# One written order of the engines from the feed-forward through the attention, with the first scores and softmax weights inside the feed-forward's end

## The chip, the cores and the metric

The kernel runs on one core of a Trainium2 chip. A core has five engines with queues of their own: PE (TensorE, matrix products into the accumulator banks of PSUM), DVE (VectorE), ACT (ScalarE), POOL (GpSimd) and SP (SyncE, which here only issues transfers). Each engine works through its queue in order and waits on semaphores for the others; sixteen DMA engines move data between DRAM and the on-chip memory. The metric is the device time of the whole kernel in microseconds (us), the median of several runs; lower is better.

## The reference

Two layers of a gated cross-attention network work on x, 4 sequences of 512 rows of 512 numbers (16 tiles of 128 rows). Each of four stages adds `tanh(gate) * f(layernorm(x))` to x:

1. a gated product with the context, whose "expert" is chosen by a row's token number;
2. a feed-forward in which rows, weights and hidden values are rounded in blocks of 32 to a small float format: `down(q(silu(gate(q(h))) * up(q(h))))`, with 2048 hidden columns;
3. an attention in which queries are the normalised x, keys and values are the context, with 8 heads that each cover 64 of a sequence's 512 rows and attend over the 512 columns: `softmax(q k / 8) v`;
4. a mixture of 64 experts, 6 per row, with at most 96 rows per expert, and a shared expert.

The change touches the end of stage 2 and stage 3.

## The kernel before, in words

**Framework.** Tiles come from pools with a number of buffers; a tile whose buffers are in use waits for a release, and a pool that opens where a closed one lay waits for what was in it. Inside `tc.manual_schedule(engines=...)` the named engines keep the order of the program; elsewhere a scheduler with an estimate of times orders them at compile time. SP is always ordered by the scheduler, and so are DMA issues on it.

**Feed-forward (lines 611 to 806).** One manual block over PE, ACT, DVE and POOL. Per tile j: `normal` (ACT) makes h; `block_scales` and `block_round` (DVE, with a wide cast on ACT, L638) round it; `turned_rows` transposes it (PE, L668, with a copy on ACT, L669); `gate_up(j, c)` computes 512 columns of gate and of up for c = 0 to 3 (PE, L688), each in a PSUM bank of its own from `ps_g` (4 banks); `silu` (ACT, L698) reads the gate bank, `times_up` (DVE, L702) multiplies with the up bank; the 1024 columns of a half are rounded and transposed (`turned_hidden`); `down` (PE, L708) makes y; `add_rows` scales it (ACT, L713) and POOL adds it to x_rows in DRAM (L714). The loop interleaves two tiles: `turned_hidden(j - 1, 1)` and `down(j - 1)` run in the round of tile j. `row_sums` on ACT (L150: an Identity and a Square pass, each with a sum) and `row_factors` on DVE give the normalisation, four tiles at a time.

**Queries of the attention.** `query_moments` uses DVE instead: `bn_stats`, `bn_aggr`, and per group three Newton steps (`newton`) for the inverse root. Groups are tiles 0 and 1, 2 and 3, then fours; the first two groups lie in rounds 13 and 14 of the feed-forward. `query(0)` (ACT) closes round 14.

**Attention (lines 831 to 1156).** A second manual block, over PE, ACT and DVE. Step n is quarter i of tile j: `scores` (PE, L850, two heads into a two-bank tile at_s, two such tiles), `highest` (DVE, L855), `weights` (ACT, L864, exponentials p, with their sums), and two steps later `turned` (PE transposes of p, L874, and copies on ACT to pT, L875). p lies in the pool `at`, which is opened after the feed-forward's pools are closed. `values`, `weighted` and `attended` of tile j - 1 follow within tile j; `attended` also sends x_tile to out (L920), and `row` makes the router's input. `fetch` loads rows of the context (c_tile, 3 buffers), `fetch_rows` loads x_rows (x_tile, 6 buffers). Expert weights are loaded on SP meanwhile (`load_expert`, L816 to L819), the first once the feed-forward's weights are done with.

**Experts.** After the attention the scheduler orders all engines again.

The functions which the change and the prediction name:

Of the kernel before, what the change touches and what calls it, by code (L numbers as in the profile page):

```python
# [9 lines left out]
F32 = mybir.dt.float32  # L10
# [4 lines left out]
ALU = mybir.AluOpType  # L15
# [4 lines left out]
P = 128  # L20
# [26 lines left out]
def flamingo_kernel(  # L47
# [101 lines left out]
            waste = pool.tile([P, D], F32, name="waste", bufs=1)  # L149
            nc.scalar.activation(waste, rows, f, bias=rows[:, 0:1], scale=-1.0, accum_out=sums[:, k, i : i + 1])  # L150

    def row_factors(small, sums, tiles):

        n = len(tiles)
        mean = small.tile([P, 2, n], F32, name="ln_mean", tag=f"ln_mean{n}")
        nc.vector.tensor_scalar(mean, sums, 1.0 / D, None, ALU.mult)
        a = small.tile([P, n], F32, name="ln_a", tag=f"ln_a{n}")
        nc.vector.scalar_tensor_tensor(a, mean[:, 0, :], -1.0, mean[:, 0, :], ALU.mult, ALU.mult)
        nc.vector.scalar_tensor_tensor(a, a, EPS, mean[:, 1, :], ALU.add, ALU.add)
        y = newton(a, small=small)  # L160
        shift = small.tile([P, n], F32, name="ln_shift", tag=f"ln_shift{n}")
        for i, rows in enumerate(tiles):
            nc.vector.scalar_tensor_tensor(
                shift[:, i : i + 1], mean[:, 0, i : i + 1], rows[:, 0:1], y[:, i : i + 1], ALU.subtract, ALU.mult
            )
        return [(y[:, i : i + 1], shift[:, i : i + 1]) for i in range(n)]
# [414 lines left out]
        nc.vector.bn_stats(st, tiles[j]["x"])  # L581
        nc.vector.bn_aggr(mv, st)

    query_groups = [[0, 1], [2, 3], [4, 5, 6, 7], [8, 9, 10, 11], [12, 13, 14, 15]]
    queries_of = {j: g for g in query_groups for j in g}

    def query_moments(j):
# [17 lines left out]
    def query(j):  # L605
        q = early.tile([P, D], F32, name="q")
        normalized(q, tiles[j]["x"], tiles[j].pop("first"))
        tiles[j]["q"] = q


    with (
        tc.tile_pool(name="ffn", bufs=2) as fp,
        tc.tile_pool(name="ffn_few", bufs=4) as few,
        tc.tile_pool(name="ps_g", bufs=4, space=PSUM) as ps_g,
        tc.tile_pool(name="ps_a", bufs=2, space=PSUM) as ps_a,
        tc.tile_pool(name="ps_h", bufs=1, space=PSUM) as ps_h,
        tc.tile_pool(name="ps_y", bufs=1, space=PSUM) as ps_y,
        tc.manual_schedule(engines={PE, ACT, DVE, POOL}),
    ):
        stages = [{} for _ in range(NT)]  # L620

# [59 lines left out]

        def gate_up(j, c):
            hT = stages[j]["hT"]
            got = []
            for wT in (wgT, wuT):
                ps = ps_g.tile([P, 512], F32, name="gu", tag="g")
                for k in range(KC):
                    nc.tensor.matmul(ps, hT[:, k, :], wT[:, k, bass.ts(c, 512)], start=k == 0, stop=k == KC - 1)  # L688
                got.append(ps)
            stages[j]["gu", c] = got  # L690

        def silu(j, c):

# [15 lines left out]
            stages[j]["y"] = y  # L709

        def add_rows(j):
            y_sb = fp.tile([P, D], F32, name="y_sb")
            nc.scalar.mul(y_sb, stages[j].pop("y"), tg_f0_256)  # L713
            nc.gpsimd.dma_start(x_rows[bass.ts(j, P), :], y_sb, accum_op=ALU.add)  # L714

# [36 lines left out]
        for j in range(NT):  # L752
            more = j + 1 < NT

            if j:
                turned_hidden(j - 1, 1)
            times_up(j, 0)
            times_up(j, 1)
            gate_up(j, 2)
            silu(j, 2)  # L760
            block_scales(j, ("a", 0), half_n)
            block_round(j, ("a", 0), half_n)
            gate_up(j, 3)
            silu(j, 3)
            if j:
                down(j - 1)
            if j + 8 < NT:
                load(j + 8)
            sums_of(j + 6)
            if j + 2 < NT:  # L770
                normal(j + 2)
            if more:
                block_scales(j + 1, "h", D)
                block_round(j + 1, "h", D)
            if j:
                add_rows(j - 1)
            if more:
                turned_rows(j + 1)
            turned_hidden(j, 0)
            if more:  # L780
                gate_up(j + 1, 0)
                silu(j + 1, 0)
            times_up(j, 2)
            times_up(j, 3)
            block_scales(j, ("a", 1), half_n)
            if more:
                gate_up(j + 1, 1)
                silu(j + 1, 1)
            block_round(j, ("a", 1), half_n)
            factors_from(j + 3)  # L790

            if j == NT - 6:
                for i in range(2):
                    fetch(i)
                for i in range(6):
                    fetch_rows(i)
            if j == NT - 3:
                query_moments(0)
                query_moments(1)
            if j == NT - 2:  # L800
                query_moments(2)
                query_moments(3)
                query(0)
        turned_hidden(NT - 1, 1)
        down(NT - 1)
        add_rows(NT - 1)
    mx_pool.__exit__(None, None, None)

# [23 lines left out]
    tp = at_pool.__enter__()  # L832
    with (
        tc.tile_pool(name="rt", bufs=2, side="right") as ap,
        tc.tile_pool(name="ps_s", bufs=2, space=PSUM) as ps_s,
        tc.tile_pool(name="ps_u", bufs=2, space=PSUM) as ps_t,
        tc.tile_pool(name="ps_o", bufs=2, space=PSUM) as ps_m,
        tc.manual_schedule(engines={PE, ACT, DVE}),
    ):
        first_w = ap.tile([P, KC, E + 2 * F], F32, name="first_w", bufs=1)  # L840

        def scores(j, i):
            t = tiles[j]
            if i == 0:
                t["pT"] = [tp.tile([P, KC, D], F32, name=f"pT{h}", bufs=1) for h in range(2)]
                t["sums"] = tp.tile([P, KC, 2], F32, name="sums")
            s = ps_s.tile([P, 2, D], F32, name="at_s")
            for h in range(2):
                rows = bass.ts(h, HD)
                nc.tensor.matmul(s[:, h, :], t["q"][rows, bass.ts(i, P)], t["c"][rows, :], start=True, stop=True)  # L850
            t["s", i] = s

        def highest(j, i):
            low = small.tile([P, 2], F32, name="low")
            nc.vector.tensor_reduce(low, tiles[j]["s", i], AX.X, ALU.max, negate=True)  # L855
            tiles[j]["low", i] = low

        def weights(j, i):

            t = tiles[j]  # L860
            s, low = t.pop(("s", i)), t.pop(("low", i))
            p = tp.tile([P, 2, D], F32, name="p", bufs=3)
            for h in range(2):
                nc.scalar.activation(  # L864
                    p[:, h, :], s[:, h, :], AF.Exp, bias=low[:, h : h + 1], accum_out=t["sums"][:, i, h : h + 1]
                )
            t["p", i] = p

        def turned(j, i):
            p = tiles[j].pop(("p", i))  # L870
            for h in range(2):
                ps = ps_t.tile([P, KC, P], F32, name="p_ps", tag="t")
                for k in range(KC):
                    nc.tensor.transpose(ps[:, k, :], p[:, h, bass.ts(k, P)], ident)  # L874
                nc.scalar.copy(tiles[j]["pT"][h][:, :, bass.ts(i, P)], ps)  # L875
# [20 lines left out]
        def bank(among, n, name):  # L896

            if among:
                return ps_m.tile([P, n], F32, name=name, tag="m")
            return ps_s.tile([P, 2, D], F32, name="at_s")[:, 0, :n]  # L900

        def values(j):
            pT = tiles[j].pop("pT")
# [170 lines left out]
        for n in range(NT * KC):  # L1074
            j, i = divmod(n, KC)
            turn = divmod(n - 2, KC)
            if i == 2:
                do(query, j + 1)
                do(weighted, j - 1)
            elif i == 3:  # L1080
                do(squashed, j - 2)
            scores(j, i)
            highest(j, i)
            do(turned, *turn)
            weights(j, i)
            if i == 0:
                do(turned_row, j - 2)
                do(over_sums, j - 1)
                do(shared_hidden, j - 3)
                do(groups_of, j - 3)  # L1090
                do(noted, j - 4, range(3))
                do(fetch, j + 2)
                if j >= 2:
                    do(fetch_rows, j + 4)
            elif i == 1:
                do(spread_sums, j - 1)
                do(experts_of, j - 3)
                do(values, j - 1)
                do(kept, j - 3)
                do(noted, j - 4, range(3, TOPK))  # L1100
                if j + 4 < NT:
                    query_moments(j + 4)
            elif i == 2:
                do(counted, j - 3)
                do(attended, j - 1)
                do(first_layer, j - 2)
                if j < ew.bufs:
                    load_expert(j, ew)
            else:
                do(slots, j - 3)  # L1110
                do(row, j - 1)
# [42 lines left out]
        noted(z, range(TOPK))  # L1154
        for j in range(z - 2, NT):
            shared_hidden(j)
    with (
        tc.tile_pool(name="ex", bufs=2) as xp,
        tc.tile_pool(name="ew3", bufs=2, side="right") as ew3,
# [146 lines left out]
```

## Time and profile before

| what | us |
|---|---|
| median of 3 runs (1237.53 to 1246.21) | 1242.14 |
| profiled execution | 1243.6 |
| its span, first to last instruction | 1241.3 |
| PE busy | 1019.4 (82%) |
| DVE busy | 798.3 (64%) |
| ACT busy | 566.2 (46%) |
| last transposes of the feed-forward (PE, L668) | start at 518.32 |
| third score step of the attention (PE, L850) | starts at 534.68 |

In rows of the timeline the columns are start, duration, engine, line, operation, output from input, shapes and count; in brackets stands the idle time of the engine before the row and what ended it. "PEld" is a weight load, "SPq" a queue's issue. In the chain of waits the columns are start, duration and what. A row of the view by stages begins with the stretch and its length, then busy us and instructions of PE, PEld, DVE, ACT and POOL, the granted PE clock, the DMA share and GB/s.

### The profile page before, as it was taken

The page shows a single profiled execution, that of the slowest core. Times are in us where ns is not written, and L with a number is a line of the kernel's source. Part 1 is how long each engine was busy: PE and PEld are TensorE (multiplying, and loading weights), DVE is VectorE, ACT ScalarE, POOL GpSimd, SP SyncE. Part 2 cuts the span into 40 slices and gives each one's busy share as a digit, 9 for nine tenths or more (in the row PEclk, how much of TensorE's full clock was granted, in tenths as well). Part 3 has the DMA queues.
Part 4 walks back from the last instruction along what each step waited for, and adds up shares of the span by engine and source line. Part 5 has one row for each costly group of instructions (what it writes and reads, how often), then busy time and mean ns, then how long its engine had stood idle before and what let it go on. Part 6 is the DMA issues. An engine that isn't in the chain of part 4 may idle for free.

```text
span 1241.3 us, 14865 instructions
## 1 busy us (share of the span) xinstructions
PE 1019.4 (82%) x4603; PEld 515.6 (42%) x4603; DVE 798.3 (64%) x1993; ACT 566.2 (46%) x1128; POOL 380.0 (31%) x526
## 2 busy tenths in 40 slices
PE   4489999637888787679999999971899999999993
PEld 4244454313333343234444444430455555544441
DVE  7799999949999999636878887762232222222231
ACT  3666674446767664366666666630111112111120
POOL 3123222100000000000544544554444444444424
PEclk9689999859999999989999999985899999999997
DMA  8934533331221111186221111027899999999978
GB/s 309 338 85 103 121 82 86 44 117 35 51 43 26 18 23 14 39 221 182 62 65 59 53 62 46 19 73 220 236 279 280 274 265 273 273 270 278 276 194 137
DMA packets 75804, 174.74 MB, mean 141 GB/s; under 512 B 13024, under 2 KB 14064, under 8 KB 75664
## 3 DMA queue, kind: packets, MB, share of 16 engines
q1 hardware_dynamic: 51696, 128.04, 34.6%
q0 software_dynamic: 23200, 45.16, 18.8%
q8 instruction: 37, 0.61, 0.2%
q10 hardware_dynamic: 832, 0.62, 0.2%
q14 instruction: 39, 0.32, 0.1%
HBM read 133.76 MB, written 44.20 MB: 143 GB/s over the span
## 4 chain that ended last, share of the span: by engine, by line
DVE 37%; PE 29%; DMA 20%; ACT 6%; issue 5%; POOL 1%; SPq 0%; DVEq 0%; POOLq 0%; ACTq 0%
DMA more_rows<-e_o,idx 13%; PE gu_ps L1196 5%; DVE mx_top L633 4%; PE e_y L1219 3%; PE first_ps L959 3%; PE at_o L907 3%; DVE inter L702 3%; DVE mx_q L649 3%; DVE low L855 3%; PE at_s L850 3%; PE l_mm L474 3%; PE p_ps L874 2%; DVE w_q L263 2%; DVE mx_c L656 2%; DVE w_src L260 2%
## 5 line engine op out<-in xcount | busy, mean ns | idle before, releaser
L1196 PE MATMUL gu_ps<-e_gu,gT 128*96 128x384 f32 x512 | 178.2, 491 | 0.0
L1200 DVE SCALAR_TENSOR_TENSOR a<-s,xg,gu_ps 96x192 f32<-96x192 f32 x64 | 35.0, 548 | 150.3 <-ACT s L1198 145.7
L1219 PE MATMUL e_y<-e_dn,eaT 96*96 96x512 f32 x256 | 120.5, 592 | 0.1
L123 POOL DMA_INDIRECT taken<-token_no,to_i x96 | 96.7, 1007 | 50.2 <-issue 24.3
L855 DVE TENSOR_REDUCE low<-at_s 128x2 f32<-128x1024 f32 x64 | 77.8, 1215 | 48.5 <-PE at_s L850 48.5
L1196 PEld LDWEIGHTS gu_ps<-e_gu,gT 128*96 128x96 f32 x512 | 79.2, 165 | 62.5 <-issue 62.2
L864 ACT ACTIVATE p<-at_s,low 128x512 f32<-128x512 f32 x128 | 87.4, 693 | 28.2 <-DVE low L855 25.1
L1188 DVE COPY gT<-g_ps 128x384 f32<-128x384 f32 x64 | 35.7, 558 | 96.8 <-PE g_ps L1186 91.6
L714 POOL DMA_DIRECT2D x_rows<-y_sb x16 | 13.7, 856 | 269.2 <-ACT y_sb L713 269.2
L1221 ACT COPY e_o<-e_y 96x512 f32<-96x512 f32 x64 | 37.2, 581 | 127.3 <-PE e_y L1219 64.4
L875 ACT COPY pT<-p_ps 128x512 f32<-128x512 f32 x128 | 70.7, 596 | 33.1 <-PE p_ps L874 32.1
L491 POOL DMA_INDIRECT x_rows<-y_sb,to_row x19 | 36.5, 1921 | 154.6 <-ACT y_sb L490 154.6
L850 PE MATMUL at_s<-c_tile,q 64*128 64x512 f32 x256 | 73.8, 655 | 11.2 <-ACT p L864 10.6
L1173 POOL DMA_INDIRECT xg<-h_rows,idx x64 | 59.9, 935 | 72.5 <-DVE a L1200 36.4
L874 PEld LDWEIGHTS p_ps<-ident,p 128*128 128x128 f32 x512 | 55.9, 143 | 59.0 <-issue 22.9
L874 PE MATMUL p_ps<-ident,p 128*128 128x128 f32 x512 | 74.8, 286 | 6.7 <-ACT hT L952 5.8
L688 PEld LDWEIGHTS <-hT 128*128 128x128 bf16 x512 | 49.8, 101 | 73.4 <-issue 17.1
L474 PE MATMUL l_mm<-cT,sT 128*128 x152 | 79.9, 674 | 0.3 <-ACT sT L461 0.3
L1198 ACT ACTIVATE s<-gu_ps 96x192 f32<-96x192 f32 x64 | 20.9, 326 | 123.0 <-PE gu_ps L1196 118.1
L688 PE MATMUL gu<-wgT,hT 128*128 128x512 bf16 x256 | 70.8, 402 | 6.1 <-ACT hT L669 6.1
L688 PE MATMUL gu<-wuT,hT 128*128 128x512 bf16 x256 | 68.1, 390 | 5.3 <-DVE inter L702 5.3
L668 PE MATMUL q_ps<-ident_bf,mx_c 128*128 128x128 bf16 x320 | 26.0, 233 | 56.1 <-DVE mx_c L656 41.1
(239 smaller groups left out, 2044.2 us busy)
## 6 DMA issues: line engine op xcount, KB each, us to landing
e_gu<-in_L_ffn_w_gate_dram SPq DMA_DIRECT2D x64, 384.0 KB
e_gu<-in_L_ffn_w_up_dram SPq DMA_DIRECT2D x64, 384.0 KB
e_dn<-in_L_ffn_w_down_dram SPq DMA_DIRECT2D x64, 384.0 KB
w_src<-in_L_ffn_w_gate_dram SPq DMA_DIRECT2D x8, 512.0 KB
c_sb<-in_ctx_dram SPq DMA_DIRECT2D x4, 1024.0 KB
w_src<-in_L_ffn_w_up_dram SPq DMA_DIRECT2D x8, 512.0 KB
more_rows<-zeros SPq DMA_DIRECT2D x16, 256.0 KB
w_src<-in_L_ffn_w_down_dram SPq DMA_DIRECT2D x8, 512.0 KB
```

The source lines that it names most:

```text
L123: ins = nc.gpsimd.indirect_dma_start(out=table[:, :], out_offset=bass.IndirectOffsetOnAxis(ap=to, axis=0), in_=what, in_offset=None)
L474: nc.tensor.matmul(ps.unsqueeze(1), aT[:, k, :], cT[:, bass.ds(at + k, 1), :], start=k == 0, stop=k == KC - 1)
L633: nc.vector.tensor_reduce(top, s3, AX.X, ALU.max, apply_absolute_value=True)
L688: nc.tensor.matmul(ps, hT[:, k, :], wT[:, k, bass.ts(c, 512)], start=k == 0, stop=k == KC - 1)
L850: nc.tensor.matmul(s[:, h, :], t["q"][rows, bass.ts(i, P)], t["c"][rows, :], start=True, stop=True)
L855: nc.vector.tensor_reduce(low, tiles[j]["s", i], AX.X, ALU.max, negate=True)
L864: nc.scalar.activation(p[:, h, :], s[:, h, :], AF.Exp, bias=low[:, h : h + 1], accum_out=t["sums"][:, i, h : h + 1])
L874: nc.tensor.transpose(ps[:, k, :], p[:, h, bass.ts(k, P)], ident)
L875: nc.scalar.copy(tiles[j]["pT"][h][:, :, bass.ts(i, P)], ps)
L1173: nc.gpsimd.indirect_dma_start(out=g[:, :], out_offset=None, in_=h_rows[:, :], in_offset=bass.IndirectOffsetOnAxis(ap=idx[:, e : e + 1], a ...
L1196: nc.tensor.matmul(ps, gT[:, k, :], gu[:, :, k, :], start=k == 0, stop=k == KC - 1)
L1219: nc.tensor.matmul(y, aT[:, c, :], dn[:, c, :], start=c == 0, stop=c == 1)
```

## The change

- One `manual_schedule` over PE, ACT and DVE spans the feed-forward and the attention; POOL is in no manual block any more.
- `ps_s` (two tiles of two banks) is opened ahead of both stages and replaces `ps_g`: gate and up of one `gate_up` share a tile, which the attention's scores use too.
- `scores`, `highest` and `weights` move ahead of the feed-forward; p and the sums lie in the pool `early`. Steps 0 and 1 of tile 0 are written between the last operations of the feed-forward, and left out of the attention's loop.
- The last tile's y_sb is a c_tile buffer of `early`.
- The moments of tiles 0 to 3 become `row_sums` on ACT in rounds 12 and 13 and one `row_factors` for four tiles in round 14, with the factor 1/8 handed on to `newton`.

```diff
-    def row_factors(small, sums, tiles):
+    def row_factors(small, sums, tiles, scale=None):
...
-        y = newton(a, small=small)
+        y = newton(a, scale, small=small)
...
-    query_groups = [[0, 1], [2, 3], [4, 5, 6, 7], [8, 9, 10, 11], [12, 13, 14, 15]]
+    query_groups = [[4, 5, 6, 7], [8, 9, 10, 11], [12, 13, 14, 15]]
...
+    def scores(j, i):
+        t = tiles[j]
+        if i == 0:
+            t["sums"] = early.tile([P, KC, 2], F32, name="sums")
+        s = ps_s.tile([P, 2, D], F32, name="at_s", tag="s")
...
+    def weights(j, i):
...
+        p = early.tile([P, 2, D], F32, name="p", bufs=3)
...
+    order = tc.manual_schedule(engines={PE, ACT, DVE})
+    order.__enter__()
+    score_banks = tc.tile_pool(name="ps_s", bufs=2, space=PSUM)
+    ps_s = score_banks.__enter__()
...
-        tc.tile_pool(name="ps_g", bufs=4, space=PSUM) as ps_g,
...
-        tc.manual_schedule(engines={PE, ACT, DVE, POOL}),
...
-            got = []
-            for wT in (wgT, wuT):
-                ps = ps_g.tile([P, 512], F32, name="gu", tag="g")
+            ps = ps_s.tile([P, 2, 512], F32, name="gu", tag="s")
+            for i, wT in enumerate((wgT, wuT)):
...
-            y_sb = fp.tile([P, D], F32, name="y_sb")
+            if j < NT - 1:
+                y_sb = fp.tile([P, D], F32, name="y_sb")
+            else:
+                y_sb = early.tile([P, D], F32, name="c_tile", bufs=3)
...
-            if j == NT - 3:
-                query_moments(0)
-                query_moments(1)
+            if j == NT - 4:
+                sums = few.tile([P, 2, 4], F32, name="ln_sums", tag="ln_sums4")
+            if NT - 4 <= j < NT - 2:
+                for i in range(2):
+                    t = 2 * (j - NT + 4) + i
+                    row_sums(fp, tiles[t]["x"], sums, t)
             if j == NT - 2:
-                query_moments(2)
-                query_moments(3)
+                for t, s in enumerate(row_factors(small, sums, [tiles[t]["x"] for t in range(4)], 1.0 / HD**0.5)):
+                    tiles[t]["first"] = s
                 query(0)
+            if j == NT - 1:
+                scores(0, 0)
+                scores(0, 1)
+        highest(0, 0)
         turned_hidden(NT - 1, 1)
+        weights(0, 0)
+        highest(0, 1)
         down(NT - 1)
+        weights(0, 1)
         add_rows(NT - 1)
...
-            scores(j, i)
-            highest(j, i)
+
+            if n >= 2:
+                scores(j, i)
+                highest(j, i)
             do(turned, *turn)
-            weights(j, i)
+            if n >= 2:
+                weights(j, i)
...
+    score_banks.__exit__(None, None, None)
+    order.__exit__(None, None, None)
```

More of the change, by code (lines that the diff above doesn't have):

```diff
@@ L608, in query, with highest @@
         tiles[j]["q"] = q
+    def scores(j, i):
[3 more added lines that the diff above has]
+        s = ps_s.tile([P, 2, D], F32, name="at_s", tag="s")
+        for h in range(2):
+            rows = bass.ts(h, HD)
+            nc.tensor.matmul(s[:, h, :], t["q"][rows, bass.ts(i, P)], t["c"][rows, :], start=True, stop=True)
+        t["s", i] = s
+    def highest(j, i):
+        low = small.tile([P, 2], F32, name="low")
+        nc.vector.tensor_reduce(low, tiles[j]["s", i], AX.X, ALU.max, negate=True)
+        tiles[j]["low", i] = low
+    def weights(j, i):
+        t = tiles[j]
+        s, low = t.pop(("s", i)), t.pop(("low", i))
+        p = early.tile([P, 2, D], F32, name="p", bufs=3)
+        for h in range(2):
+            nc.scalar.activation(
+                p[:, h, :], s[:, h, :], AF.Exp, bias=low[:, h : h + 1], accum_out=t["sums"][:, i, h : h + 1]
+            )
+        t["p", i] = p
+    order = tc.manual_schedule(engines={PE, ACT, DVE})
+    order.__enter__()
+    score_banks = tc.tile_pool(name="ps_s", bufs=2, space=PSUM)
+    ps_s = score_banks.__enter__()
     with (
@@ L683, in gate_up @@
             hT = stages[j]["hT"]
-            got = []
-            for wT in (wgT, wuT):
-                ps = ps_g.tile([P, 512], F32, name="gu", tag="g")
+            ps = ps_s.tile([P, 2, 512], F32, name="gu", tag="s")
+            for i, wT in enumerate((wgT, wuT)):
                 for k in range(KC):
-                    nc.tensor.matmul(ps, hT[:, k, :], wT[:, k, bass.ts(c, 512)], start=k == 0, stop=k == KC - 1)
-                got.append(ps)
-            stages[j]["gu", c] = got
+                    nc.tensor.matmul(ps[:, i, :], hT[:, k, :], wT[:, k, bass.ts(c, 512)], start=k == 0, stop=k == KC - 1)
+            stages[j]["gu", c] = ps[:, 0, :], ps[:, 1, :]
         def silu(j, c):
@@ L834, in flamingo_kernel, with turned @@
         tc.tile_pool(name="rt", bufs=2, side="right") as ap,
-        tc.tile_pool(name="ps_s", bufs=2, space=PSUM) as ps_s,
         tc.tile_pool(name="ps_u", bufs=2, space=PSUM) as ps_t,
         tc.tile_pool(name="ps_o", bufs=2, space=PSUM) as ps_m,
-        tc.manual_schedule(engines={PE, ACT, DVE}),
     ):
         first_w = ap.tile([P, KC, E + 2 * F], F32, name="first_w", bufs=1)
-        def scores(j, i):
-            t = tiles[j]
+        def turned(j, i):
             if i == 0:
[L845 to L869, printed above, removed]
+                tiles[j]["pT"] = [tp.tile([P, KC, D], F32, name=f"pT{h}", bufs=1) for h in range(2)]
             p = tiles[j].pop(("p", i))
@@ L899, in bank @@
                 return ps_m.tile([P, n], F32, name=name, tag="m")
-            return ps_s.tile([P, 2, D], F32, name="at_s")[:, 0, :n]
+            return ps_s.tile([P, 2, D], F32, name="at_s", tag="s")[:, 0, :n]
         def values(j):
```

## The prediction

> **What bounds the kernel now.** I read the page's slices first: PE's row falls to 7, 6 and 7 tenths in the three slices from 465 to 558 us, where the feed-forward hands over to the attention. The chain of waits over that stretch says why:
>
> ```profile
> 510.58 1.29 DVE inter L702 x2
> ...
> 514.80 1.14 DVE low L855
> 515.94 0.60 DVE mx_c L655
> 516.59 0.99 issue
> 517.59 0.69 DVE mx_c L656
> 518.32 0.62 PE q_ps L668 x8
> 518.94 5.15 PE y L708 x16
> 524.12 0.70 ACT y_sb L713
> ...
> 525.10 6.70 DMA x_rows<-y_sb
> 531.89 1.28 ACT L864
> 533.18 1.46 ACT p L864 x4
> 534.68 2.08 PE at_s L850 x4
> ...
> 554.08 10.65 DMA out_dram<-x_tile
> 564.80 2.62 DMA x_tile<-x_rows
> ```
>
> Columns: start, us, what. The two score maxima (low) are already computed at 514.7, inside the last rounding, and delay it. The exponentials (p) stand ready from 518 on but wait for the last feed-forward rows to be added in DRAM, then for a table load; PE's third score step waits for them until 534.68. Twenty us later DVE waits 5.2 us for x_tile 6, whose buffer is free only when out of tile 0 has landed.
>
> Then the timeline of DVE, ACT, PE and SP, for durations and slack:
>
> ```profile
> 482.09 0.69 DVE L581 BATCH_NORM_STATS2 st<-x_tile 128x6 f32<-128x512 f32 x1
> 486.47 1.28 DVE L702 TENSOR_TENSOR inter<-inter,gu 128x512 f32<-128x512 f32 x2
> ```
> ```profile
> 274.98 0.71 ACT L150 ACTIVATE waste<-xt 128x512 f32<-128x512 f32 x1
> 275.59 0.19 ACT L150 ACTIVATION_READ_ACCUMULATOR waste<-xt 128x1 f32 x1
> ```
> ```profile
> 476.57 0.84 PE L668 MATMUL q_ps<-ident_bf,mx_c 128*128 128x128 bf16 x12 [0.87 <-DVE mx_c L656]
> 495.01 1.30 PE L668 MATMUL q_ps<-ident_bf,mx_c 128*128 128x128 bf16 x12 [3.32 <-DVE mx_c L656]
> 496.13 1.89 PE L688 MATMUL gu<-wgT,hT 128*128 128x512 bf16 x4
> 499.09 1.03 PE L688 MATMUL gu<-wgT,hT 128*128 128x512 bf16 x4
> ```
> ```profile
> 246.76 1.59 SPq L571 DMA_DIRECT2D c_tile<-in_ctx_dram  x3
> ```
>
> DVE is packed in the feed-forward: the pair of L702 recurs after 14.07 us (448.29 to 462.36) without a gap, while PE waits 0.87 us for it. So DVE time saved there counts. After a gap of 3.3 us PE runs at half speed for some 3.4 us (1.89 against 1.03 for four matmuls).
>
> **DVE part, tiles 12 to 14.** Each removed set of moments plus Newton steps took 4.38 us (482.09 to 486.47) and 4.39 us (500.53 to 504.92). Added on DVE: one row_factors for four tiles. For three it took 3.25 us (265.72 to 268.97); a fourth shift and the scale multiply add 0.2 each: 3.65. Net -5.12.
>
> Added on ACT: two passes for each of four tiles, 0.85 us from start to start with the read-out, 3.4 us in tile 12 and again in 13. Cover in tile 12: ACT is free at 466.98; +3.4 = 470.4; copy of iT to 471.3; activation to 471.9; wide cast to 472.9, wanted by DVE at 473.08; third activation to 473.4; normalising tile 15 to 474.15, wanted at 473.69. So 0.46 us shows. Tile 13 has no normalising behind the sums: 0. Without that cover the cost would be 6.8. The multiplies of tile 15 start at 504.92 - 5.12 + 0.46 = 500.26 instead of 504.92.
>
> **Shared banks.** Gate and up now share one two-bank tile, free only after times_up, where a gate bank was free after its activation. Behind gate_up(j,2) stand PE's down(j-1) and the next transposes, for which ACT and then DVE wait. In a plain tile the multiply ends 0.65 us after the pair starts, and gate_up ran at 468.62, 0.59 after the pair at 468.03: 0.1 us, inside the 0.87. With factors ahead of the pair (tiles 1, 5, 9) PE now idles before gate_up instead of before q_ps; half speed costs 1.7 either way, and the next activation comes at the same point: 0, bounds 0 and +1 each.
>
> Tile 14 differs: query(0) waits for the factors, and PE idles from 497.3 to 500.95 (3.6 us). Half speed, the nearest row being the 3.32 gap: gate/up (2) and (3) end at 506.05 (4 x 0.87 + 1.7), down(14) at 509.5, transposes 510.1; ACT's y_sb 510.25, iT 511.2, wide cast 512.15. DVE would want that cast at 500.26 + 5.66 + 5.05 = 510.97: a new stall of 1.2 (none if full speed is kept). The last mx_c then ends at 512.9, against 518.27: the maxima, 2.03 us on the chain, have left its path.
>
> **The transition.** PE: both scores 510.1 to 512.2, transposes 513.0 to 513.6, ACT's copy to 514.6. The gap is 0.8 us instead of 4.42, so down(15) runs at 0.22 a matmul (3.62, as in the plain tiles, not 5.30): begun at 513.5, it ends at 517.1 instead of 524.08, and the copy is there before its second half (515.3). DVE: highest(0,0) ends 514.1. ACT: table 514.6 to 515.9, four exponentials of 0.67 to 518.6, the first two at 517.25. No DMA stands before them, because p is in the early pool. Third scores: 517.3 against 534.68, -17.4.
>
> One added wait: y_sb of tile 15 takes a c_tile buffer, and SP filled all three at 246.76. Then add_rows(15) waits for the last read of c_tile 0, scores(0,3), at 517.3 + 1.06 + 1.02 + 1.06 = 520.4. ACT stands there; queued behind are query(1) and the copies of p, for which PE's transposes wait. Copies end at 520.45 + 0.69 + 0.72 + 1.07 = 522.9 (521.1 without the wait); before, weights(0,2) began behind them at 539.17. Gain 16.3, bounds 16.3 and 18.1; I take 16.3, since that SP row shows the buffers taken. The add itself has no early reader. POOL, no longer bound by order, issues only the sixteen adds: 0. The larger early pool shifts feed-forward tiles in memory; xt waits for the last weight transposes (250.92) now, so -2.5 to 0: I take 0.
>
> **Next bottleneck: x_tile 6.** out of tile 0 is ready at 553.15 - 16.3 = 536.9. SP issues expert loads (1.18 MB each), first_w and the rest in an order fixed at compile time. In the trace out stands behind five and two thirds experts and lands after 10.65 us. The Trainium skill ("DMA: Bandwidth & Descriptors", "Anatomy of one DMA") gives a lone DMA about 2 us fixed plus bytes over 436 GB/s: 2.6 us for 256 KB, which would erase the stall and gain 16.3 + 5.2 = 21.5. The row shows it queued in a full stream, so I keep 10.65: the stall stays 5.2 and the gain 16.3. This needs fewer loads in front. first_w no longer waits for the add (532.13 becomes about 518.5), and the third scores come 10.4 us sooner relative to expert 0's loads and 3.8 sooner relative to first_w; at one issue per us, which 23 transfers in the 22 us before out amount to, three to ten loads should fall behind, and five (2 MB, 9 us) are enough. With the old order, 8.5 MB (expert 0's 1.18 and the 7.35 behind it) must pass from 517; at 225 GB/s, the rate of those 7.35 MB from 532.1 to 564.8, out lands at 555, 10 us sooner than 564.80.
>
> **Does it reach the end?** Attention is 94% PE (17.0 of 18 us in 690 to 708), and the experts load as their buffers free up:
>
> ```profile
> 900.00:950.00 50.00, 50.00 (x192) 25.45 (x191) 14.56 (x33) 9.65 (x21) 24.77 (x22) 1.00 1.06 282
> ```
> PE and DMA are full, and both start from the attention's end: passed on one to one; +-3 for a reordered expert stage.
>
> **Sum.** The profiled execution took 1243.6 (span 1241.3 and 2.3 outside it), 1.5 above the median of 1242.14. 1243.6 - 16.3 = 1227.3, less 1.5: 1226.
>
> **Rivals.** Likeliest, 0.48: as summed, 1226 (1222 to 1230).
> Old transfer order, 0.21: the stall at x_tile 6 grows to about 12, gain 10: 1232. For it: transfers were saturated from 540 on. Against: SP's order follows readiness.
> out passes the loads, 0.12: stall gone, 1220.5.
> The exponentials gain nothing, because pT's memory or the y_sb buffer still ties ACT to the adds, 0.09: only DVE's 5 us remain, 1237.
> Slower, 0.10: the shared banks take PE's lead. Each pair may be released 1.05 us later (second activation done 466.98, wanted 468.03) before DVE waits one for one. Half-speed PE over a whole tile costs 48 matmuls x 0.21 = 10 us. If the wait opened a 3.3 us gap in most tiles, 15 tiles losing 2 us would cost 30, less 16: 1256 or more. It decides at 1.1 us a tile. Against: the multiplies come directly at the pair's start, 0.1 us late.
>
> **Numbers.** About 1% is what a measurement of this kernel can tell from no change; 1% is 12.4 us. Faster by more: 0.43 + 0.12 + 0.03 = 0.58. Within: 0.05 + 0.18 + 0.08 = 0.31. Slower: 0.11. Range 1219 to 1241: it leaves out the slower case and a few hundredths of each tail.
>
> **What would show it.** The first exponential follows the table load with no wait on x_rows; third scores near 517; the pair of tile 15 near 500.3; copies of p near 523; out landing near 547 and DVE's stall on x_tile about 5. Wrong if PE's idle before q_ps vanishes in plain tiles and the pair's 14.07 us grows, if the stall at x_tile 6 doubles, or if the expert stage changes its length.

## The result and the profile after

The kernel after took 1226.62 us (median of 12 runs, 1219.84 to 1235.36) and the kernel before 1240.51 (12 runs, 1235.96 to 1246.21; the 1242.14 from which the forecast started was the median of three). The ratio is 0.9895, 95% interval 0.987 to 0.992: 13.0 us less, between 9.9 and 16.1; the medians alone differ by 13.9. The profiled execution after took 1232.19 (span 1230.4), 5.6 over its median, so the profiles alone differ by 11.4 and the spans by 10.9.

The forecast of 1226 is met, but several of its terms are not, and the gain that it stood for, 16.1 us, lies at the edge of the interval. The table follows both profiles from landmark to landmark (us from the start of the span). mx_c are the rounded values, and over_ps is PE's spread of the inverse sums, which comes once in each attention tile.

| landmark | before | after | moved | forecast |
|---|---|---|---|---|
| first multiplies of the feed-forward, tile 0 | 273.69 | 274.83 | +1.1 | 0 |
| multiplies of tile 12 begin | 453.96 | 460.27 | +6.3 | 0 |
| first multiplies of tile 15 | 504.92 | 506.69 | +1.8 | -4.7 |
| last mx_c ends | 518.27 | 519.49 | +1.2 | -5.4 |
| third scores | 534.68 | 524.03 | -10.7 | -17.4 |
| first over_ps of attention tile 0 | 545.38 | 533.36 | -12.0 | -16.3 |
| x_tile 6 is issued | 564.80 | 552.30 | -12.5 | -16.3 |
| first over_ps of attention tile 3 | 599.30 | 591.52 | -7.8 | -16.3 |
| first product of the experts | 874.93 | 866.64 | -8.3 | -16.3 |
| end of the span | 1241.3 | 1230.4 | -10.9 | -16.3 |

**The transition did what it was meant to do.** Busy time by engine over the hand-over, first before, then after; after the name of the stretch come its length, then PE, PEld, DVE, ACT and POOL with busy us and instructions, then the granted clock, DMA share and GB/s:

```profile
510.00:560.00 50.00, 31.43 (x163) 16.16 (x164) 21.62 (x32) 25.94 (x56) 3.98 (x14) 0.86 0.67 164
```
```profile
510.00:560.00 50.00, 44.67 (x251) 22.43 (x248) 29.20 (x45) 35.42 (x77) 4.23 (x15) 0.99 0.68 185
```

PE works 13 us more of these 50, at a clock of 0.99 instead of 0.86. The timeline of the kernel after, all engines (start, duration, engine, line, operation; in brackets the idle time before it and what ended it):

```profile
512.46 0.69 DVE L687 TENSOR_TENSOR mx_c<-mx_c,mx_wide 128x1024 bf16<-128x1024 bf16 x1 [0.81 <-ACT mx_wide L669]
...
518.80 0.69 DVE L687 TENSOR_TENSOR mx_c<-mx_c,mx_wide 128x1024 bf16<-128x1024 bf16 x1 [0.78 <-ACT mx_wide L669]
...
520.01 3.62 PE L737 MATMUL y<-wdT,iT 128*128 128x512 bf16 x16
...
521.24 1.28 ACT L631 ACT_TABLE_LOAD   x1
...
522.53 0.69 ACT L631 ACTIVATE p<-at_s,low 128x512 f32<-128x512 f32 x1
...
524.03 1.13 PE L617 MATMUL at_s<-c_tile,q 64*128 64x512 f32 x4 [0.41 <-ACT p L631]
...
525.20 0.70 ACT L746 ACTIVATE c_tile<-y,factors 128x512 f32<-128x512 f32 x1
...
526.48 1.09 ACT L891 COPY pT<-p_ps 128x512 f32<-128x512 f32 x2
```

Where the chain before had 6.70 us of DMA ahead of the exponentials, the table load now follows ACT's copy of 520.21 (1.01 us) directly, and the first exponential follows it. The last product of down runs at full speed (3.62). From the last mx_c to the third scores it is 4.5 us, where it was 16.4. add_rows of tile 15 (525.20) does not wait either. SP's timeline shows why:

```profile
246.43 0.81 SPq L571 DMA_DIRECT2D c_tile<-in_ctx_dram  x2
...
523.70 0.62 SPq L1080 DMA_DIRECT2D first_w<-in_L_ffn_gate_w_dram  x1
...
527.28 0.33 SPq L571 DMA_DIRECT2D c_tile<-in_ctx_dram  x1
...
542.14 0.34 SPq L936 DMA_DIRECT2D out_dram<-x_tile  x1
...
552.30 0.33 SPq L576 DMA_DIRECT2D x_tile<-x_rows  x1
```

SP fetches two c_tile buffers early and not three (246.76, x3, before): the third is y_sb's, and its fetch comes at 527.28.

**What came late before that: the feed-forward.** The shared banks were to cost nothing. Who waited for whom on the gate and up products, before, then after (us, times):

```profile
who waited for it (us, times):
  ACT inter L698: 13.4, 29
...
  PE gu L688: 5.3, 5
```
```profile
who waited for it (us, times):
  ACT inter L727: 56.0, 58
...
  PE gu L718: 13.5, 4
```

ACT's activation now waits for PE almost every time, 42.6 us more in all. The products behind the second multiplies of a tile show the form of it, first before (tile 12), then after (tile 14):

```profile
463.57 1.04 PE L688 MATMUL gu<-wgT,hT 128*128 128x512 bf16 x4 [0.23 <-ACT hT L669]
464.45 1.03 PE L688 MATMUL gu<-wuT,hT 128*128 128x512 bf16 x4
...
464.65 0.60 ACT L698 ACTIVATE inter<-gu 128x512 f32<-128x512 f32 x1 [0.22 <-PE gu L688]
```
```profile
498.73 1.04 PE L718 MATMUL gu<-wgT,hT 128*128 128x512 bf16 x4 [0.23 <-ACT hT L700]
499.61 1.03 PE L718 MATMUL gu<-wuT,hT 128*128 128x512 bf16 x4
...
500.67 0.60 ACT L727 ACTIVATE inter<-gu 128x512 f32<-128x512 f32 x1 [1.08 <-PE gu L718]
```

Before, the activation of the gate half began 1.08 us after the gate product had begun, while the up product ran. After, it begins 1.94 us later, when the up product is done too, though it reads nothing of it.

In the plain rounds the later activation costs nothing: DVE's pair of multiplies recurs after 14.07 us as before (446.20 to 460.27). From the first multiplies to those of tile 12 the kernel after loses 5.2 us, 2.0 of them in the first tile and 3.2 net around the three rounds in which row_factors stand ahead of the multiplies. There PE had a lead in the kernel before, shown first: the activation (364.32) and three of the four products of such a round began before the multiplies, and only the last product waited for a bank. After, PE waits for the multiplies before it can begin any of the four:

```profile
364.32 0.60 ACT L698 ACTIVATE inter<-gu 128x512 f32<-128x512 f32 x1
...
365.90 1.28 DVE L702 TENSOR_TENSOR inter<-inter,gu 128x512 f32<-128x512 f32 x2
...
366.64 1.02 PE L688 MATMUL gu<-wuT,hT 128*128 128x512 bf16 x4 [0.64 <-DVE inter L702]
```
```profile
370.33 1.28 DVE L731 TENSOR_TENSOR inter<-inter,gu 128x512 f32<-128x512 f32 x2
...
371.08 1.89 PE L718 MATMUL gu<-wgT,hT 128*128 128x512 bf16 x4 [3.42 <-DVE inter L731]
...
374.69 0.60 ACT L727 ACTIVATE inter<-gu 128x512 f32<-128x512 f32 x1 [6.00 <-PE gu L718]
...
376.26 0.69 DVE L687 TENSOR_TENSOR mx_c<-mx_c,mx_wide 128x1024 bf16<-128x1024 bf16 x1 [0.97 <-ACT mx_wide L669]
```

The activation came 1.6 us before the multiplies and now comes 4.4 after them, and DVE then waits 0.97 us for the wide cast behind it. An estimate from these rows: had the activation begun when the gate product ended (372.97), the cast would have been done 1.7 us sooner, before DVE wanted it. By this estimate the loss there needs both, banks that come free late and a wait for both products.

**What came late behind it: a second stall.** DVE's waits for x_tile in the kernel after, and then PE's next router product, first after, then before:

```profile
555.04 0.70 DVE L581 BATCH_NORM_STATS2 st<-x_tile 128x6 f32<-128x512 f32 x1 [5.16 <-DMA x_tile<-x_rows]
...
574.27 0.69 DVE L581 BATCH_NORM_STATS2 st<-x_tile 128x6 f32<-128x512 f32 x1 [2.80 <-DMA x_tile<-x_rows]
```
```profile
578.62 4.97 PE L975 MATMUL first_ps<-first_w,hT 128*128 128x448 f32 x8 [4.22 <-DVE r L931]
```
```profile
588.09 3.27 PE L959 MATMUL first_ps<-first_w,hT 128*128 128x448 f32 x8 [0.99 <-DVE r L915]
```

The wait for x_tile 6 is what it was before (5.18). A second one, for x_tile 7, opens PE's gap to 4.22 us, behind which the router runs at about half speed (a granted clock of 0.66 from 578.62 to 583.59; 1.00 in the kernel before). 4.22 less 0.99, and 4.97 less 3.27: 4.9 us, which is what attention tile 2 loses (23.90 us from its first over_ps to the next tile's, 18.98 before). From there nearly all that is left reaches the experts.

### The profile page after: what moved, and what is told of

Same layout as the page of the kernel before. It is cut to its first block, busy times and chain, and to the rows that moved or that the text cites. A ratio compares the mean times of both kernels' runs of the same rounds, so it can differ in the third digit from the quotient of the medians.

```text
span 1230.4 us, 14849 instructions
## 1 busy us (share of the span) xinstructions
PE 1018.0 (83%) x4603; PEld 512.5 (42%) x4603; DVE 792.9 (64%) x1976; ACT 572.3 (47%) x1144; POOL 385.4 (31%) x526
## 5 line engine op out<-in xcount | busy, mean ns | idle before, releaser
L747 POOL DMA_DIRECT2D x_rows<-y_sb x15 | 12.9, 863 | 262.1 <-ACT y_sb L746 262.1
L718 PE MATMUL gu<-wgT,hT 128*128 128x512 bf16 x256 | 72.0, 407 | 20.7 <-DVE inter L731 13.5
L491 POOL DMA_INDIRECT x_rows<-y_sb,to_row x19 | 39.5, 2081 | 150.3 <-ACT y_sb L490 150.3
L1243 POOL DMA_INDIRECT out_dram<-e_o,idx x34 | 48.8, 1435 | 117.3 <-ACT e_o L1242 51.8
L474 PE MATMUL l_mm<-cT,sT 128*128 x152 | 75.1, 641 | 0.0
L474 PE MATMUL l_mm<-cT,hT 128*128 x152 | 71.4, 614 | 1.9 <-ACT hT L461 1.9
```

Of the source, the lines that this page charges most:

```text
L474: nc.tensor.matmul(ps.unsqueeze(1), aT[:, k, :], cT[:, bass.ds(at + k, 1), :], start=k == 0, stop=k == KC - 1)
L718: nc.tensor.matmul(ps[:, i, :], hT[:, k, :], wT[:, k, bass.ts(c, 512)], start=k == 0, stop=k == KC - 1)
L1243: nc.gpsimd.indirect_dma_start(out=tables[e % 2 if e < E - LAST else 0][:, :], out_offset=bass.IndirectOffsetOnAxis(ap=idx[:, e : e + 1], ...
```

## Experiments

After the result stood three theories. **A**: the shared banks cost some 6 us in the feed-forward, since waits go by the whole two-bank tile. **B**: the move of the first scores and exponentials out of the way of the DRAM adds is worth 12 us by itself, and the sums on ScalarE 5 to 8. **C**: x_tile's turn-round (out of tile j, then the load of tile j+6 behind expert loads) takes part of the gain back. The rivals: banks that cost nothing and an offset by chance; a gain that is all from the sums; a stall that moves on, whatever the buffers.

Each experiment has runs of the kernel before made with it, on one of three chips, and these differ (medians 1240.22, 1240.85 and 1236.56). So gains are given from the ratio to before, and two experiments are compared by their ratios. Landmarks come from one profiled execution of each.

### The shared banks alone, on the kernel before

```diff
-            got = []
-            for wT in (wgT, wuT):
-                ps = ps_g.tile([P, 512], F32, name="gu", tag="g")
+            ps = ps_g.tile([P, 2, 512], F32, name="gu", tag="g")
+            for i, wT in enumerate((wgT, wuT)):
...
-        tc.tile_pool(name="ps_g", bufs=4, space=PSUM) as ps_g,
+        tc.tile_pool(name="ps_g", bufs=2, space=PSUM) as ps_g,
```

> Before, with gate and up in one two-bank tile and nothing else changed. By the record (a pair is free 0.1 us later, inside PE's slack) the time stays within 0 to +3 us of before. By the reading of the changed kernel's trace (the activation now waits for both products, and tiles with factors or moments ahead of the multiplies lose PE's lead) the feed-forward grows by 6 to 9 us: 2.6 in the first two tiles, about 1 in each of the three tiles with factors, 1 to 1.5 in each of the two with moments.

1241.90 us, ratio 1.0016 (0.9988 to 1.0044): no difference that can be told, where a loss of up to 5.5 us would be inside the interval. The trace shows a cost all the same: from the first multiplies to the last pair it takes 243.37 us (273.36 to 516.73), before 236.89. Of these 6.5 us 3.8 are left when ACT's exponentials begin (537.0 and 533.2), 3.7 at the first over_ps of attention tile 0 (549.09 and 545.38), and 3.4 at the last over_ps of the attention (821.96 and 818.55). At the experts' first product none is left (874.85 and 874.93), but the stretch between is the one whose length differs among all profiles (see Open). So the cost is there, a part of it was absorbed before the exponentials, and that the rest vanished is not shown.

### The sums on ScalarE alone, on the kernel before

```diff
-            if j == NT - 3:
-                query_moments(0)
-                query_moments(1)
+            if j == NT - 4:
+                sums = few.tile([P, 2, 4], F32, name="ln_sums", tag="ln_sums4")
+            if NT - 4 <= j < NT - 2:
+                for i in range(2):
+                    t = 2 * (j - NT + 4) + i
+                    row_sums(fp, tiles[t]["x"], sums, t)
...
```

> Before, with the moments of tiles 0 to 3 as sums on ACT and nothing else changed. By the record DVE gains 5.1 us and loses 0.5 behind ACT: -4.7 us, which reach the end. Rival: ACT or the transition gives it back (PE's new gap in tile 14, the wait for x_tile 6), and less than 2 us are left.

1231.15 us, ratio 0.9936 (0.991 to 0.9962): 7.9 us less (4.7 to 11.2). First multiplies to last pair: 232.37, 4.5 less than before; the first over_ps comes 4.9 sooner (540.49) and the last 5.1 (813.47). What the time shows beyond that lies behind the attention. The exponentials still wait for the DRAM adds, as ACT's timeline shows:

```profile
526.86 1.28 ACT L867 ACT_TABLE_LOAD   x1 [6.87 <-DMA x_rows<-y_sb]
```

### Gate and up in banks of their own, on the kernel after

Four banks serve gate and up as before, and are given back just before the first scores, which take two tiles of two banks in their place.

```diff
+    gate_banks = tc.tile_pool(name="ps_g", bufs=4, space=PSUM, side="right")
...
-            ps = ps_s.tile([P, 2, 512], F32, name="gu", tag="s")
+            got = []
+            for wT in (wgT, wuT):
+                ps = ps_g.tile([P, 512], F32, name="gu", tag="g")
...
             if j == NT - 1:
+                gate_banks.__exit__(None, None, None)
+                score_banks = tc.tile_pool(name="ps_s", bufs=2, space=PSUM, side="right")
...
                 scores(0, 0)
```

> After, with gate and up in banks of their own (the four banks are given back before the first scores). If the shared tile is what made the feed-forward of the changed kernel 5.8 us longer up to tile 12, those come back: about -19 us against before, and the activation starts 1.1 us after its gate product's start again. If the growth has another cause (the one written order, other addresses), the time stays at about -13.5.

1219.83 us, ratio 0.9828 (0.9795 to 0.9861): 21.3 us less than before, 8.3 less than after. First multiplies to last pair: 231.98, against 238.24 after. The products' waiters are those of before again:

```profile
who waited for it (us, times):
  ACT inter L729: 14.2, 30
```

The 6.3 us reach the first over_ps (526.69, after 533.36), and by that of tile 3 the lead is 9.6 (581.94), since the second stall is smaller too. The interval lies clear of that of the kernel after (0.987 to 0.992). This shows A.

### Waits by the tile: the activation between the two products

Here the gate's activation is issued between the gate and the up product of the shared tile.

```diff
             for i, wT in enumerate((wgT, wuT)):
                 for k in range(KC):
                     nc.tensor.matmul(ps[:, i, :], ...)
+                if i == 0:
+                    silu(j, c)
...
```

> After, with each activation written between the gate and the up product, in the shared tile. If waits go by tile, the up product now waits for the activation: PE's 12 us a tile grow by four waits of about 1 us, past DVE's 14.07 in many tiles, 10 to 30 us slower than after. If they go by bank, the activation starts 0.87 us sooner at no price, and 3 to 5 us of the 5.8 come back: about -17 against before. If the late release alone is what costs, nothing changes: -13.5.

1245.16 us, ratio 1.0037 (1.0011 to 1.0062): some 18 more than after. The waits before the instructions on the products, in this kernel:

```profile
its engine sat idle before it (us, times) until:
  PE gu L719: 65.2, 65
  ACT inter L729: 48.7, 64
```

PE now waits for the activation in all 64 pairs, though it writes the half that the activation does not read. In the kernel after the activation waits for the second product, in this one the second product waits for the activation: the two halves of one tile are ordered as if they were one piece. That is what a shared tile adds and two tiles do not; how much of the 6 us is due to this and how much to the later release of banks, no run separates.

### The order alone: banks apart, moments on DVE

The kernel with gate and up in banks of their own, with its sums undone: DVE takes the moments again.

```diff
-            if NT - 4 <= j < NT - 2:
-                for i in range(2):
-                    t = 2 * (j - NT + 4) + i
-                    row_sums(fp, tiles[t]["x"], sums, t)
...
+            if j == NT - 3:
+                query_moments(0)
+                query_moments(1)
...
```

> a_sep with the moments on DVE as before: the written order and the transition alone, without shared banks and without sums on ACT. If the parts add up, it is slower than a_sep by what the sums alone gained (4.7 by the record, 7.9 in the run of the sums alone): -13 to -16 against before. If the sums' gain and the transition's overlap, -18 or better.

1228.95 us, ratio 0.9905 (0.9872 to 0.9938): 11.8 us less than before. With the sums added (21.3) the two make about what they make apart, 11.8 + 7.9 = 19.7. The first over_ps comes at 532.52, 12.9 sooner than before; by attention tile 3 (591.47) it is 7.8 sooner, with DVE waiting 8.0 us for x_tile. Both parts of B are real. The order's is the larger at the first over_ps (12.9 against 4.9); by the times the two intervals overlap. No run separates, within the order, the place of p in memory from the earlier place of the first scores.

### Seven x_tile buffers, with the banks apart

```diff
-        xt = early.tile([P, D], F32, name="x_tile", bufs=6)
+        xt = early.tile([P, D], F32, name="x_tile", bufs=7)
...
-            best = ap.tile([P, GRP, 8], F32, name="best")
+            best = ap.tile([P, GRP, 8], F32, name="best", bufs=1)
```

> The version with banks of their own (a_sep), with seven x_tile buffers instead of six (and one buffer less of a small router tile, for the room). If DVE's stalls on x_tile 6 and 7 (3.8 and 2.0 us in a_sep's trace) and PE's half speed after them are on the path, they go: 5 to 8 us faster than a_sep, about -27 against before. If the rows then queue behind the expert loads all the same, or PE is the next limit at once, less than 2 us come of it.

1215.41 us, ratio 0.9793 (0.9766 to 0.9821): 25.7 us less than before and the best of all kernels here, ahead of before and after. DVE waits for no x_tile. From the first over_ps of tile 0 to that of tile 3 it takes 53.96 us, with six buffers 55.25. Against the same kernel with six buffers the intervals overlap, so the buffer's own share, 4 us by the ratios and 1.3 in these traces, is likely and not proven.

### Seven x_tile buffers, on the kernel after

The same edit, with the banks shared:

```diff
-        xt = early.tile([P, D], F32, name="x_tile", bufs=6)
+        xt = early.tile([P, D], F32, name="x_tile", bufs=7)
...
```

> The kernel after with seven x_tile buffers, and one buffer for the tile best to make room. If the two waits of DVE for x_tile 6 and 7 are what keeps the shared-bank kernel from its full gain (5.2 and 2.8 us in its profile, with 4.9 us lost in the second), the attention's end comes 5 to 9 us sooner and the time is about 1219, ratio to before 0.979 to 0.985. If the queue of expert loads in front of the transfers sets the pace whatever the number of buffers (the stall only moves to another tile), it stays within 2 us of the kernel after, ratio 0.988 to 0.991.

1223.28 us, ratio 0.9869 (0.9811 to 0.9928): 3 us under after by the ratios, which these intervals can't tell from no change, and between the two forecasts. The trace is plainer: tile 0 to tile 3 takes 53.16 us against 58.16, and the statistics for tile 7 start without a wait.

```profile
572.93 0.68 DVE L581 BATCH_NORM_STATS2 st<-x_tile 128x6 f32<-128x512 f32 x1
```

So the second stall is the lack of a buffer, and the queue does not move it on. Of the 5.0 us, 2.0 are not seen at the end because this execution reached attention 2.0 later (535.32 against 533.36); the other 3.0 are there at tile 3 (588.48 against 591.52), and 3.8 at the experts (862.80 against 866.64).

### Out on the other queue

With banks apart, out of the attention is issued on ScalarE's queue, so that it does not stand behind SP's expert loads.

```diff
-            nc.sync.dma_start(out[bass.ts(j, P), :], xt)
+            nc.scalar.dma_start(out[bass.ts(j, P), :], xt)
```

> a_sep with the attention's out transfers issued by ACT instead of SP, so on another ring. If out's 10 us come from its place behind the loads on SP's ring, it lands in 2 to 4 us now, and x_tile 6 follows sooner, as far as it is not itself queued behind loads: 0 to 5 us faster than a_sep. If the shared engines are what it waits for, out still takes about 10 us and the time is a_sep's.

1226.38 us, ratio 0.989 (0.9848 to 0.9932): some 7 us more than with out on SP, though the two intervals just overlap. In the traces attention tile 3 comes 4.2 later (586.10 against 581.94), from a first over_ps at the same time. The timelines of the hand-over of x_tile 6, first with out on SP, then on ACT's queue:

```profile
534.49 0.34 SPq L941 DMA_DIRECT2D out_dram<-x_tile  x1
...
544.25 0.33 SPq L576 DMA_DIRECT2D x_tile<-x_rows  x1
...
547.04 0.69 DVE L581 BATCH_NORM_STATS2 st<-x_tile 128x6 f32<-128x512 f32 x1 [3.85 <-DMA x_tile<-x_rows]
```
```profile
534.58 0.35 ACTq L941 DMA_DIRECT2D out_dram<-x_tile  x1
...
542.97 0.33 SPq L576 DMA_DIRECT2D x_tile<-x_rows  x1
...
549.03 0.70 DVE L581 BATCH_NORM_STATS2 st<-x_tile 128x6 f32<-128x512 f32 x1 [5.88 <-DMA x_tile<-x_rows]
```

Out is done sooner, 8.4 us after its issue and not 9.8, but the load that follows it takes 6.1 us until DVE starts and not 2.8. With out on SP, SP issued nothing from 536.25 until x_tile 6, and the DMA engines' busy share while x_tile 6 was loaded was 0.79 (544.3 to 547.1). With out on the other queue SP sent one expert load more (at 538.13), and the share was 1.04, full, throughout (542.9 to 549.1). What is won on one half of the turn-round is more than lost on the other. That the expert loads are what delays x_tile 6 is argued from the order of issue; the share of each transfer was not measured.

### The last y_sb in the feed-forward's pool, on the kernel after

```diff
-            if j < NT - 1:
-                y_sb = fp.tile([P, D], F32, name="y_sb")
-            else:
-                y_sb = early.tile([P, D], F32, name="c_tile", bufs=3)
+            y_sb = fp.tile([P, D], F32, name="y_sb")
```

> After, with the last y_sb in the feed-forward's pool again (p stays in the early pool). By the record only p's place ties the exponentials to the add, so they run at the same time; but what lies where the feed-forward's pool lay (pT, first_w) should wait for the add: copies of p begin 6 to 8 us later, and about -7 against before is left. Rival: a wait goes by the tiles that really overlap, and the time is that of after, -13.

1230.51 us, ratio 0.9919 (0.9896 to 0.9943), 3 us over after by the ratios, with overlapping intervals. The exponentials are not touched. The copies of p are:

```profile
528.65 1.07 ACT L887 COPY pT<-p_ps 128x512 f32<-128x512 f32 x2 [3.80 <-DMA x_rows<-y_sb]
```

The first over_ps comes at 536.26, 2.9 later than after; then the wait for x_tile is gone, and attention tile 3 comes at 590.01, 1.5 sooner than after. In the traces the c_tile buffer for y_sb saves a wait here, and the later stall takes it back.

## Why the prediction held, step by step

**DVE's part, tiles 12 to 14: right in sum, its cover misjudged.** row_factors for four tiles took 3.51 us (503.18 to 506.69), forecast 3.65. From the first multiplies of tile 12 to those of tile 15 it takes 5.3 us less than before, with the sums alone (45.66 against 50.96) and with banks apart (45.67): the 0.46 us that ACT's sums were to cost in tile 12 show in neither. In the kernel after it takes 46.42, 4.5 less (forecast 4.66), because DVE waits 0.46 and 0.47 us for a wide cast behind the two rounds of sums; behind the second nothing had been forecast.

**Shared banks: the step that failed.** "Half speed costs 1.7 either way, and the next activation comes at the same point: 0, bounds 0 and +1 each." That PE would now idle before gate_up was right: its waits for the multiplies are four (13.5 us), three behind the factors and one in tile 14. That the next activation comes at the same point was wrong, for two reasons. Before, PE had run ahead of the multiplies in these rounds, so the activation had come before them; this lead was counted as nothing. And the activation may start only when both products are done, 0.86 us later at full clock; this was not considered. By tile 12 the kernel after had lost 5.2 us from the first multiplies on and 0.7 more up to them, and with banks apart all but 0.5 of this is gone. The rival for slower named the right place and too large a price: 6 us in all is under 0.5 a tile, where 1.1 was needed.

**Tile 14: right in form.** PE waited 3.48 us for the multiplies behind the factors, and then ran at half speed, as its timeline shows; in place of one stall of 1.2 DVE had two, 0.81 and 0.78. With banks apart PE waited 1.74 us there and DVE not at all, so these stalls are the banks' too.

```profile
507.43 1.72 PE L718 MATMUL gu<-wgT,hT 128*128 128x512 bf16 x4 [3.48 <-DVE inter L731]
...
508.95 1.91 PE L718 MATMUL gu<-wuT,hT 128*128 128x512 bf16 x4
```

**The transition: right.** Third scores 4.5 us after the last mx_c, forecast 4.4 (517.3 less 512.9). They came 6.7 later than forecast, all of it from ahead of this stage: 5.8 of the banks (0.5 of it shows with banks apart too), 0.5 of an earlier stage and 0.4 of DVE's second stall in tile 14.

**y_sb's wait: wrong, and cheaper than taken.** I let SP's three c_tile fetches of the kernel before stand for the order of the kernel after, though the buffer for y_sb is one of the three and its place in the rotation is fixed by the program. SP fetched two, and nothing waited. The copies ended 3.5 us after the third scores (forecast 5.6), so the upper bound of 18.1 was the one to take.

**x_tile 6: right, with out's old latency.** Out to x_tile 6 took 10.16 us (forecast 10.65), the stall 5.16 (5.2). The rule weighed against the row, a lone transfer's 2.6 us from the Trainium skill ("DMA: Bandwidth & Descriptors", "Anatomy of one DMA"), would have erased the stall; the row was the right guide. That section's fit is for transfers issued by GpSimd, and out is issued by SP behind others; the load of x_tile 6 behind it did take 2.62 us in the kernel before. Seven loads fell behind out; three to ten were forecast, five were needed.

**What was missed: x_tile 7.** The same turn-round one tile later took 10.22 us (558.30 to 568.52), before 8.01 (570.71 to 578.72). In the kernel before there was slack for it; now there was not, and 4.9 us were lost. I had followed the first stall to its end and not asked whether the next buffer in the rotation was any better off.

**The sum.** At the first over_ps: 16.3 forecast, less 0.5 of an earlier stage, less 5.8 for banks, less 0.4 in tile 14, plus 2.1 because the copies of p end 3.5 and not 5.6 us after the third scores (1.8 of it the wait that did not come), is 11.7; 12.0 was measured. Less 4.9 for x_tile 7 and plus 0.7 at the tiles around it gives 7.8. Another 0.5 came back up to the experts and 2.6 between there and the end, inside the 3 that were allowed. The profile thus shows 10.9 where 16.3 was forecast; the medians differ by 13.9, since after's profiled execution lay 5.6 over its median and before's 3.1. So the time was hit in part by luck: errors of both signs cancelled, the forecast started 1.6 us above the later median of before, and single executions scatter.

**Open.** From attention's last over_ps to the experts' first product the profiles take between 52.4 us (banks apart) and 56.4 (before), without order by the change; one execution of each can't say whether that is scatter. It bears on every landmark at the experts above. The 3.2 us that after gained behind the last expert product were not followed either.

## What to carry to other kernels

Two results in one on-chip tile shared their waits in both directions here, even where each lay in a bank of its own, and an engine that had run ahead lost its lead; before merging buffers, ask not only when they come free but which reader now waits for which writer. When a stall is removed or moved, follow every later use of the same rotation of buffers, not only the next one, with the slack that each had. A gain in an early stage counts where it arrives at the stage that is full: of 6.5 us lost in the feed-forward of one kernel 3.4 were left at the attention's end, too few to be told in its time, while 6.3 in another went with 8 us of time.

## What was not expected of the hardware

A transfer moved from a full queue to an empty one finished 1.4 us sooner (8.4 against 9.8), and the load issued next on the full queue took 3.3 us longer; the attention lost 4.2 us by tile 3 and the kernel some 7. PE's half speed came again after a gap of 4.22 us and cost 1.7 us on eight matmuls of 128x448 (granted clock 0.66); after the gap of 0.99 us in the kernel before the same eight ran at a granted clock of 1.00.
